# Half of an output projection by Strassen's seven products, in a new order of the stage's close

## The chip, the cores and the metric

The kernel runs on one core of one Trainium2 chip. Its metric is device time in microseconds (us); the time before is the median of three runs, 615.01 us (614.92 to 615.44). The core's engines have queues of their own and run beside each other: PE (TensorE, matrix products, with a loader for the stationary operand that the profile calls PEld), DVE (VectorE), ACT (ScalarE), POOL (GpSimd) and SP (SyncE, which here only issues transfers). In this kernel PE's products go into PSUM, used as eight banks of 128 x 512 floats, and DVE or ACT read them from there; POOL works on the other on-chip memory, SBUF.

## The reference, cut to what matters

512 tokens (8 sequences of 64) of width 512 go through three layers, each added to its input:

```python
x = x + xattn(layernorm(x), ctx, W, b)        # attention over 1601 context rows
x = x + attn(layernorm(x), ...)               # linear attention, then an MLP
x = x + ffn(layernorm(x), ...)                # 8 experts, top 2

# attn: 16 heads of 64, causal
h = _ln(x, g1, beta1)
q = elu((h @ wq) @ proj) + 1;  k = elu((h @ wk) @ proj) + 1;  v = h @ wv
out_t = sum_{s<=t} (q_t . k_s) v_s / (sum_{s<=t} q_t . k_s + 1e-6)
x = x + out @ wo                              # out: 512 x 1024, wo: 1024 x 512
x = x + gelu(_ln(x, g2, beta2) @ w1 + b1) @ w2 + b2
```

The change is about `x + out @ wo`. Everything is in 32-bit floats.

## The kernel before, in words

The kernel is written in a layer (Tile) that inserts the semaphores between engines. With `manual_schedule` every engine, SP's queue too, runs its instructions in the order of the program text, so the order of the Python calls below is the order of each queue. Two things come on top of that. PSUM is two pools of four banks, `mm_bank` and `acc_bank`; a new bank is the one of its pool that came free first, by the order planned when the program is built, and its first writer waits for the last reader of the tile that had it. Big inputs stream through a ring of 12 buffers of 1 MB: `stream` lists them in order, `issue_to` issues transfers up to a place in that list as long as the oldest of the 12 has been marked done (`done`), `need` asks for one and looks `AHEAD` = 6 further, and `scratch` takes a ring buffer for intermediate results.

The linear attention works on pairs of heads, j = 0 to 7, 128 channels each. Per pair:

- `linear(which, i)` projects q or k for two pairs by Strassen's seven quarter products (PE; copies on ACT L782; sums on POOL L786), with sums of weight quarters made by `sum_weights` (POOL, L719 to L722).
- `features(j)` (L821) multiplies by `proj` into two "acc" banks, `pr_wq` and `pr_wk`; ACT (L832, L836) and DVE (L838) make phi of it. phi has one buffer for each of q and k.
- `products(j)` (L851) makes the scores of 64 by 64 blocks into two "mm" banks; DVE masks them (L860) into `masked`, which has two buffers, one for each head.
- `attend_j(j)` (L874, L884) multiplies by ones and by v, into two "acc" banks `nd`.
- `denominators` (ACT, L897) and `divide` (DVE: a reciprocal of 128 x 512, L904, and two products, L906) write the pair's 128 channels of `a_t`, 512 tokens wide. The products are the last readers of the `nd` banks.

The loop over j is staggered: in round j come linear(j), attend_j(j-3), products(j-2), divide(j-3), features(j-1). So three rounds are left for the close. There the output product is worked in between: `output(t, js)` (L946) multiplies `a_t[:, j, tile t]` by the j-th 128 rows of wo, 512 columns wide, for four tiles t of 128 tokens, and adds up eight j in one PSUM bank. Before, its calls come in the order

```python
output(0, range(4)); rest = features(7); rest(0); rest(1); products(6)
output(1, range(2)); divide(5, attend_j(5)); output(1, [2, 3]); output(0, [4])
both = attend_j(6); products(7); divide(6, both); output(1, [4])
output(0, [5]); output(1, [5]); divide(7, attend_j(7)); output(2, range(6))
output(0, [6, 7]); output(1, [6, 7])   # then the joins
```

`join(t)` (DVE, L981) adds a tile's bank to the residual `xin` and takes its statistics (L983), `normal(t)` (L993) normalizes it, `turn_h2(t)` (PE, L1007) transposes it, and ACT (L996) or, for tile 2, DVE (L999) scales it. Tile 2's last two matmuls, and the whole of tile 3, stand between these. `sum_tokens` (POOL for the first tile of each half, DVE for the second, L581 to L584) makes the sums of h2 that the MLP's Strassen products need; `first_products`, `second_products` and `fifth` (L1042) are the first of these on PE. `first_products(0)` is called right behind tile 3's last output matmul, and join(3) behind it.

In the close POOL makes the sums of the first two w1 blocks (`sum_weights("w1", 0)` and 1) and of four pairs of w2 rows (`sum_down`, L745 to L748), which are used later; it is then idle until sum_tokens.

At the very start, `NIDLE` = 23 products of the identity with itself (L237) are run before there is any data; the first `NARROW` = 13 are 8 columns wide, the other ten 128.

Of the kernel before, what the change touches and what calls it, by code (L numbers as in the profile page):

```python
# [17 lines left out]
ALU = mybir.AluOpType  # L18
AX = mybir.AxisListType

P = 128
B, S, D = 8, 64, 512
# [18 lines left out]
NBIG = 7  # L41
LN_EPS = 1e-5
RING = 12
NIDLE = 23
NARROW = 13
AHEAD = 6


# [1 line left out]
def perceiver_kernel(  # L50
# [22 lines left out]
    nc = tc.nc  # L73
# [45 lines left out]
    half = H * DH // 2  # L119
# [57 lines left out]
    place = {key: i for i, (key, _) in enumerate(order)}  # L177
# [30 lines left out]
    def done(*keys):  # L208

        freed.update(keys)  # L210
# [514 lines left out]
    HD = D // 2  # L725
    scratches, dsums, hsums = {}, {}, {}

    def sums_tile(name, i):

        if (name, i // 2) not in scratches:  # L730
            scratches[name, i // 2] = scratch(f"{name}_{i // 2}")
        return scratches[name, i // 2][1][:, 2 * (i % 2) : 2 * (i % 2) + 2, :].rearrange(
            "p a (b n) -> p (a b) n", b=2
        )

    def down_part(i, row, half):

        f = 2 * i + row
        return streamed["w2", f // 4][:, f % 4, half * HD : (half + 1) * HD]

    def sum_down(i):

        s = sums_tile("dsum", i)
        t1, t2, t3, t4 = dsums[i] = [s[:, k, :] for k in range(4)]
        nc.gpsimd.tensor_tensor(t1, down_part(i, 0, 1), down_part(i, 0, 0), ALU.subtract)  # L745
        nc.gpsimd.tensor_tensor(t2, down_part(i, 1, 1), t1, ALU.subtract)
        nc.gpsimd.tensor_tensor(t3, down_part(i, 1, 1), down_part(i, 0, 1), ALU.subtract)
        nc.gpsimd.tensor_tensor(t4, down_part(i, 1, 0), t2, ALU.subtract)  # L748

    if True:  # L750
        a_t = la1.tile([P, H * DH // P, B * S], F32, name="a_t")
# [63 lines left out]
        def features(j):  # L815

            pr = {which: acc_bank(f"pr_{which}_{j}") for which in ("wq", "wk")}
            for r in range(2):
                rows = slice(r * DH, (r + 1) * DH)
                for which, other in (("wq", r), ("wk", 1 - r)):  # L820
                    nc.tensor.matmul(  # L821
                        pr[which][other * DH : (other + 1) * DH, :],
                        proj2[rows, :],
                        lin[which, j][rows, :],
                        start=True,
                        stop=True,
                    )
# [12 lines left out]
            return rest  # L840

        def products(j):


            banks_ = [mm_bank(f"qk_{j}_{r}") for r in range(2)]
            for t in range(NT):
                for h in range(2):
                    cols = slice(t * P + h * S, t * P + (h + 1) * S)
                    for r in range(2):
                        rows = slice(r * DH, (r + 1) * DH)  # L850
                        nc.tensor.matmul(  # L851
                            banks_[r][h * S : (h + 1) * S, t * S : (t + 1) * S],
                            phi["wk", j][rows, cols],
                            phi["wq", j][rows, cols],
                            start=True,
                            stop=True,
                        )
# [35 lines left out]
        def denominators(j, both):  # L893

            rden = la2.tile([P, 2, NT * S], F32, tag="rden", name=f"rden_{j}")
            for h in range(2):
                nc.scalar.activation(rden[:, h, :], both[h][:, NT * S :], AF.Identity, bias=tiny)  # L897
            return rden

        def divide(j, both, rden=None):  # L900

            if rden is None:
                rden = denominators(j, both)
            nc.vector.reciprocal(rden, rden)  # L904
            for h in range(2):
                nc.vector.tensor_tensor(  # L906
                    a_t[:, j, :].rearrange("p (t h q) -> p t h q", t=NT, h=2)[:, :, h, :],
                    both[h][:, : NT * S].rearrange("p (t q) -> p t q", t=NT),
                    rden[:, h, :].rearrange("p (t q) -> p t q", t=NT),
                    ALU.mult,  # L910
                )

        halves_of = [(which, i) for i in range(nj // 2) for which in ("wq", "wk")]
# [22 lines left out]
        for i in range(2):  # L936
            sum_weights("w1", i)
        for i in range(ND):
            sum_down(i)
        wo_banks = {}  # L940

        def output(t, js):
            if t not in wo_banks:
                wo_banks[t] = (mm_bank if t < 3 else acc_bank)(f"wo_{t}")
            for j in js:
                nc.tensor.matmul(  # L946
                    wo_banks[t],
                    a_t[:, j, t * P : (t + 1) * P],
                    wo_r[j // 4][:, j % 4, :],
                    start=(j == 0),  # L950
                    stop=(j == nj - 1),
                )

        output(0, range(4))
        rest = features(nj - 1)
        for k in range(2):
            rest(k)
        products(nj - 2)
        output(1, range(2))
        divide(nj - 3, attend_j(nj - 3))  # L960
        output(1, range(2, 4))
        output(0, [4])
# [12 lines left out]


        h2n, h2_t = v_sb[:, :, :D], v_sb[:, :, D:]
# [55 lines left out]
    mlp2 = mid.enter_context(tc.tile_pool(name="mlp2", bufs=2))  # L1033
# [1088 lines left out]
```

## Time and profile before

| what | before |
|---|---|
| median of three runs | 615.01 us (614.92 to 615.44) |
| profiled execution | 615.04 us, its span 613.3 us |
| mean granted clock of PE | 0.996 |
| PE busy | 599.7 us, 3820 instructions |
| DVE, ACT, POOL busy | 185.7, 151.2, 176.1 us |
| output product L946 | 64 matmul instructions of 128 x 512, 237.0 to 272.6 us |
| reciprocals L904 | 8 of 128 x 512, 3.34 us each |

The span runs from the first to the last instruction of one execution. A line of the timeline gives start, busy time, engine, source line, operation, output <- inputs, form and count; what stands in brackets is how long the engine had been idle before it and what ended that. A 32-bit matmul is two PE instructions, each with a load of its own on PEld, and the start-to-start distance of these in a run, not their listed duration, is what a matmul costs. Busy time of an engine says nothing by itself of what sets the end: a line counts if PE, or what PE waits for, would be later by it.

### The profile page before, as it was taken

To read this page: it belongs to the slowest core of one execution; us is meant where nothing else is said; L and a number is where in the kernel's file an instruction comes from. 1 tells how busy PE (TensorE), PEld (TensorE's weight loads), DVE (VectorE), ACT (ScalarE), POOL (GpSimd) and SP (SyncE) were. 2 spreads that over 40 slices of the span, in tenths; PEclk is the share of its full clock that TensorE was granted. 3 is DMA by queue.
4 is the path that set the end of the run, shared out by engine and by line. 5 is a ranking of instruction groups with operands and counts; after the bars stand their busy time and mean duration, and the time that the engine had idled before them with its cause. 6 is when DMAs were issued, how large, how long until landed. Compare 5 with 4: busy or idle time off the path is not lost. (4 is left out here: it accounts for less than half of the span.)

```text
span 613.3 us, 9571 instructions
## 1 busy us (share of the span) xinstructions
PE 599.7 (98%) x3820; PEld 394.4 (64%) x3820; DVE 185.7 (30%) x448; ACT 151.2 (25%) x317; POOL 176.1 (29%) x241
## 2 busy tenths in 40 slices
PE   8999999999999999999999999999999999999994
PEld 7543434343477775558888658939763848776793
DVE  4121414234402667865104245412212011101100
ACT  3241313140136665233112311301101101101110
POOL 4000000000188758415996021332300111301111
PEclk9999999999999999999999999999999999999998
DMA  8999999999822003001336414158860778775611
GB/s 333 418 418 421 418 419 415 421 418 409 341 70 69 1 3 138 2 1 34 105 138 261 151 69 149 64 162 320 286 253 1 266 270 292 287 286 179 276 20 17
DMA packets 23942, 131.87 MB, mean 215 GB/s; under 512 B 4372, under 2 KB 4372, under 8 KB 12488
## 3 DMA queue, kind: packets, MB, share of 16 engines
q1 hardware_dynamic: 19496, 122.36, 50.8%
q0 software_dynamic: 3280, 7.61, 5.1%
q10 hardware_dynamic: 1104, 1.07, 0.5%
q8 instruction: 40, 0.66, 0.4%
q14 instruction: 22, 0.18, 0.1%
HBM read 126.08 MB, written 4.94 MB: 214 GB/s over the span
## 5 line engine op out<-in xcount | busy, mean ns | idle before, releaser
L1619 PEld LDWEIGHTS up<-xgT,e_up 128*128 128x128 f32 x896 | 100.7, 192 | 4.5 <-ACT y_sb L1597 2.5
L1619 PE MATMUL up<-xgT,e_up 128*128 128x128 f32 x896 | 101.6, 276 | 1.0 <-PEq L1952 0.6
L1598 POOL DMA_INDIRECT out_dram<-y_sb,dst_late x12 | 18.3, 1526 | 167.8 <-ACT y_sb L1597 97.7
L1585 DVE TENSOR_TENSOR mid<-up,act 128x256 f32<-128x256 f32 x38 | 16.1, 425 | 150.5 <-ACT act L1583 150.5
L1633 PE MATMUL y<-e_wo,mid 128*128 128x512 f32 (+1 forms) x144 | 58.8, 548 | 0.0
L472 PE MATMUL sc<-ctxT,pw_t 128*64 128x401 f32 (+1 forms) x256 | 47.5, 503 | 0.0
L1583 ACT ACTIVATE act<-up 128x256 f32<-128x256 f32 x38 | 14.6, 383 | 119.3 <-PE up L1619 97.1
L533 PE MATMUL av<-ctx,eT 128*64 128x512 f32 x192 | 43.5, 595 | 0.0
L581 POOL TENSOR_TENSOR h_sums<-h_t 128x256 f32<-128x256 f32 x1 | 0.7, 724 | 144.1 <-PE avt L560 144.1
L1633 PEld LDWEIGHTS y<-e_wo,mid 128*128 128x128 f32 x144 | 25.7, 190 | 20.5 <-issue 17.8
L472 PEld LDWEIGHTS sc<-ctxT,pw_t 128*64 128x64 f32 x256 | 18.6, 136 | 27.2 <-issue 24.3
L1042 PE MATMUL side<-v_sb,sum_w 128*128 128x256 f32 x128 | 30.5, 380 | 0.2 <-DVE v_sb L581 0.2
L533 PEld LDWEIGHTS av<-ctx,eT 128*64 128x64 f32 x192 | 13.6, 137 | 25.3 <-issue 24.9
L946 PE MATMUL wo<-wo,a_t 128*128 128x512 f32 x64 | 29.2, 601 | 0.0
L618 PE MATMUL v<-wv,h_t 128*128 128x512 f32 x64 | 29.1, 597 | 0.0
L904 DVE RECIPROCAL rden<-rden 128x512 f32<-128x512 f32 x8 | 26.7, 3343 | 0.2 <-ACT rden L897 0.2
L1042 PEld LDWEIGHTS side<-v_sb,sum_w 128*128 128x128 f32 x128 | 24.2, 190 | 3.9 <-issue 0.6
L1127 PE MATMUL mlp<-w,hid_sb 128*128 128x512 f32 (+1 forms) x50 | 22.3, 584 | 0.0
L480 ACT ACTIVATE scores<-sc,pb 128x401 f32<-128x401 f32 (+1 forms) x16 | 9.5, 591 | 46.6 <-PE sc L472 46.6
L618 PEld LDWEIGHTS v<-wv,h_t 128*128 128x128 f32 x64 | 11.6, 190 | 13.4 <-issue 13.0
L489 DVE TENSOR_REDUCE negmax<-scores 128x1 f32<-128x1601 f32 x4 | 7.3, 1821 | 42.5 <-ACT scores L480 42.5
L946 PEld LDWEIGHTS wo<-wo,a_t 128*128 128x128 f32 x64 | 11.5, 190 | 13.2 <-issue 11.0
(353 smaller groups left out, 917.3 us busy)
## 6 DMA issues: line engine op xcount, KB each, us to landing
e_up<-in_L_ffn_up_dram SPq DMA_DIRECT2D x32, 1024.0 KB, 6.0
ctx<-in_ctx_dram SPq DMA_DIRECT2D x24, 1024.0 KB, 15.7
ctxT<-in_ctx_T_dram SPq DMA_DIRECT2D x24, 802.0 KB, 13.8
e_wo<-in_L_ffn_wo_dram SPq DMA_DIRECT2D x16, 1024.0 KB, 10.1
w<-in_L_attn_w_dram SPq DMA_DIRECT2D x8, 1024.0 KB, 8.3
ctxT<-in_ctx_T_dram SPq DMA_DIRECT2D x8, 796.0 KB, 15.3
wv<-in_L_attn_wv_dram SPq DMA_DIRECT2D x2, 1024.0 KB, 14.0
wq<-in_L_attn_wq_dram SPq DMA_DIRECT2D x2, 1024.0 KB, 15.6
```

Source lines behind the costliest of these rows:

```text
L472: nc.tensor.matmul(sc[h * S : (h + 1) * S, :width], pw_t[:, c, (2 * t + h) * S : (2 * t + h + 1) * S], keys[h][:, c, :], start=(c == 0), s ...
L533: nc.tensor.matmul(av[h * S : (h + 1) * S, :], e_t[:, 4 * g + j, h * S : (h + 1) * S], rows[h][:, j, :], start=(g == 0 and j == 0), stop=F ...
L618: nc.tensor.matmul(bank, h_t[:, c, t * P : (t + 1) * P], wv_n[:, c, :], start=(c == 0), stop=(c == KC - 1))
L904: nc.vector.reciprocal(rden, rden)
L946: nc.tensor.matmul(wo_banks[t], a_t[:, j, t * P : (t + 1) * P], wo_r[j // 4][:, j % 4, :], start=(j == 0), stop=(j == nj - 1),)
L1042: nc.tensor.matmul(bank[:, :HT], weights[:, c, :], rows[:, c, :], start=(first and c == 0), stop=(c == 1), skip_group_check=True,)
L1127: nc.tensor.matmul(acc[t][:, part], hid[:, t * P : (t + 1) * P], w[:, part], start=False, stop=(f == FF // P - 1), skip_group_check=True,)
L1583: nc.scalar.activation(act, bank[:, :FQ], AF.Silu)
L1585: nc.vector.tensor_tensor(hid, bank[:, FQ:], act, ALU.mult)
L1598: nc.gpsimd.indirect_dma_start(out=out, out_offset=bass.IndirectOffsetOnAxis(ap=dst[:n, :], axis=0), in_=y_sb[:n, :], in_offset=None, boun ...
L1619: nc.tensor.matmul(bank[:, m * P : (m + 1) * P], up_of[q][:, c, m * P : (m + 1) * P], xg_t[c], start=(c == 0), stop=(c == KC - 1),)
L1633: nc.tensor.matmul(bank[:, :width], h_t[:, j * P : (j + 1) * P], w[:, 2 * (q % 2) + j, n * width : (n + 1) * width], start=(q + j == 0), s ...
```

## The change

The first four of the eight j (two pairs of j, `NS` = 2) are multiplied by wo by Strassen's seven products instead of eight. With two j as the inner halves, two halves of 256 tokens as rows and two halves of 256 columns of wo, each product is, for one pair and one tile of 128 tokens, a matmul of 256 columns.

- Four sums of wo's quarters (`sums_of_output`) and four of a_t's (`sum_attended`) for each pair, all on POOL and in rounds 4 to 7 of the loop, into two buffers of the ring ("wo_sums") that are listed with no source.
- Products 1, 5, 6, 7 (`output_shared`) go to a bank each and serve more than one output quarter. ACT copies each to a part of `h_t`, whose old content is no longer needed, and POOL adds them to the residual `xin` in seven adds of 128 x 512. Product 7 takes an "acc" bank, the others "mm" banks.
- Products 2, 3, 4 (`output_alone`) go straight to the output banks. The last four j are multiplied as before, `output(t, [4..7])`.
- The order of the close is new: products(7) comes ahead of attend_j(6), tile 2's and tile 3's product 4 comes after chunk 7 of tiles 0 and 1, and only four chunks of tile 3 stand between the turns.
- `sum_weights("w1", ...)` and `sum_down` on POOL move behind or between the new sums and adds.
- `NIDLE` goes from 23 to 11 and `NARROW` from 13 to 1: ten wide ones remain, and one narrow one.

```diff
-NIDLE = 23
-NARROW = 13
+NIDLE = 11
+NS = 2
+NARROW = 1
...
     for r in range(2):
         stream(("wo", r), wo[r])
+    for i in range(NS):
+        stream(("wo_sums", i), None)
...
+    def columns_sums(part, outs, which=range(4)):
+        t1, t2, t3, t4 = outs
+        for k in which:
+            dst, a, b = (
+                (t1, part(0, 1), part(0, 0)),
+                (t2, part(1, 1), t1),
+                (t3, part(1, 1), part(0, 1)),
+                (t4, part(1, 0), t2),
+            )[k]
+            nc.gpsimd.tensor_tensor(dst, a, b, ALU.subtract)
...
+        def sums_of_output(i, which=range(4)):
+            if len(wo_sums) == i:
+                issue_to(place["wo_sums", i] + 1)
+                s = streamed["wo_sums", i]
+                parts_ = [s[:, k // 2, k % 2 * HD : (k % 2 + 1) * HD] for k in range(8)]
+                wo_sums.append(parts_[:4])
+                at_sums.append(parts_[4:])
+            columns_sums(lambda row, half: wo_part(i, row, half), wo_sums[i], which)
...
+        def sum_attended(i):
+            s1, s2, s3, s4 = at_sums[i]
+            even, odd = a_t[:, 2 * i, :], a_t[:, 2 * i + 1, :]
+            nc.gpsimd.tensor_tensor(s1, even[:, HT:], odd[:, HT:], ALU.add)
+            nc.gpsimd.tensor_tensor(s2, s1, even[:, :HT], ALU.subtract)
+            nc.gpsimd.tensor_tensor(s3, even[:, :HT], even[:, HT:], ALU.subtract)
+            nc.gpsimd.tensor_tensor(s4, odd[:, :HT], s2, ALU.subtract)
...
+            if j in (nj - 4, nj - 3):
+                sums_of_output(0, range(2) if j == nj - 4 else range(2, 4))
+            if j == nj - 2:
+                sum_attended(0)
+                sums_of_output(1)
+            if j == nj - 1:
+                sum_attended(1)
             if j > 2:
                 both = attend_j(j - 3)
...
+        def output_alone(k):
+            rows, weights = {
+                2: (lambda i: block(i, 1, 0), lambda i: wo_part(i, 1, 0)),
+                3: (lambda i: at_sums[i][3], lambda i: wo_part(i, 1, 1)),
+                4: (lambda i: block(i, 1, 1), lambda i: wo_sums[i][3]),
+            }[k]
+            half = int(k == 3)
+            for t in range(2):
+                output(t + 2 * (k == 4), range(NS), slice(half * HD, (half + 1) * HD), rows, weights)
...
+        def output_shared(k, pairs):
+            if k not in wo_shared:
+                wo_shared[k] = (acc_bank if k == 7 else mm_bank)(f"wo_shared_{k}")
+            for i in pairs:
+                rows = {1: block(i, 0, 0), 5: at_sums[i][0], 6: at_sums[i][1], 7: at_sums[i][2]}[k]
+                weights = {1: wo_part(i, 0, 0), 5: wo_sums[i][0], 6: wo_sums[i][1], 7: wo_sums[i][2]}[k]
+                for t in range(2):
+                    nc.tensor.matmul(
+                        wo_shared[k][:, t * HD : (t + 1) * HD],
+                        rows[:, t * P : (t + 1) * P],
+                        weights,
...
+        def copy_shared(k):
+            nc.scalar.copy(wo_copies[k], wo_shared[k].rearrange("p (t n) -> p t n", t=2))
...
+        output_shared(1, every)
+        copy_shared(1)
+        sum_weights("w1", 0)
+        add((0, 0), p1)
+        rest = features(nj - 1)
+        output_shared(5, every)
+        for k in range(2):
+            rest(k)
+        copy_shared(5)
+        output_shared(6, [0])
+        products(nj - 2)
+        both = attend_j(nj - 3)
+        rden = denominators(nj - 3, both)
+        output_shared(6, range(1, NS))
+        copy_shared(6)
+        sum_weights("w1", 1)
+        add(p6, p1)
+        add(p5, p6)
+        add((0, 1), p5)
+        add((1, 1), p5)
+        add((1, 0), p6)
+        divide(nj - 3, both, rden)
+        output_shared(7, every)
+        copy_shared(7)
+        add((1, 0), p7)
+        add((1, 1), p7)
         for i in range(ND):
             sum_down(i)
...
+        products(nj - 1)
         both = attend_j(nj - 2)
-        products(nj - 1)
         divide(nj - 2, both)
-        output(1, [4])
+        output_alone(2)
+        output_alone(3)
         for t in range(2):
-            output(t, [5])
+            output(t, [4])
         divide(nj - 1, attend_j(nj - 1))
...
-        output(2, range(6))
         for t in range(2):
-            output(t, [6, 7])
+            output(t, [5])
+        output(2, [4, 5])
+        for j in (6, 7):
+            for t in range(2):
+                output(t, [j])
+        output_alone(4)
...
         of = join(2)
-        output(3, range(3))
+        output(3, [4, 5])
         normal(2, *of)
         turn_h2(0, [by_act])
         turn_h2(1, [by_act])
-        output(3, range(3, nj - 2))
+        output(3, [6])
         turn_h2(2, [by_dve])
-        output(3, range(nj - 2, nj))
+        output(3, [7])
+        done(*[("wo_sums", i) for i in range(NS)])
```

More of the change, by code (lines that the diff above doesn't have):

```diff
@@ L743, in sum_down @@
         s = sums_tile("dsum", i)
[L744 to L748, printed above, removed]
+        dsums[i] = [s[:, k, :] for k in range(4)]
+        columns_sums(lambda row, half: down_part(i, row, half), dsums[i])
     if True:
@@ L911, in divide, with wo_part @@
                 )
+        wo_sums, at_sums = [], []
+        def sums_of_output(i, which=range(4)):
[6 more added lines that the diff above has]
+            columns_sums(lambda row, half: wo_part(i, row, half), wo_sums[i], which)
+        def wo_part(i, row, half):
+            j = 2 * i + row
+            return streamed["wo", j // 4][:, j % 4, half * HD : (half + 1) * HD]
+        def sum_attended(i):
[5 more added lines that the diff above has]
+            nc.gpsimd.tensor_tensor(s4, odd[:, :HT], s2, ALU.subtract)
         halves_of = [(which, i) for i in range(nj // 2) for which in ("wq", "wk")]
@@ L935, in perceiver_kernel, with output @@
         done(*[(which, n) for which in ("wq", "wk") for n in range(2)])
-        for i in range(2):
-            sum_weights("w1", i)
+        wo_banks = {}
+        def output(t, js, part=slice(0, D), rows=None, weights=None):
+            start = t not in wo_banks
+            if start:
+                wo_banks[t] = (mm_bank if t < 3 else acc_bank)(f"wo_{t}")
+            for j in js:
+                if rows is None:
+                    row, weight = a_t[:, j, t * P : (t + 1) * P], wo_r[j // 4][:, j % 4, :]
+                else:
+                    row, weight = rows(j)[:, t % 2 * P : (t % 2 + 1) * P], weights(j)
+                nc.tensor.matmul(
+                    wo_banks[t][:, part],
+                    row,
+                    weight,
+                    start=(start and j == js[0]),
+                    stop=(rows is None and j == nj - 1),
+                    skip_group_check=True,
+                )
@@ new lines, in block @@
+        def block(i, row, side):
+            return a_t[:, 2 * i + row, side * HT : (side + 1) * HT]
+        def output_alone(k):
[7 more added lines that the diff above has]
+                output(t + 2 * (k == 4), range(NS), slice(half * HD, (half + 1) * HD), rows, weights)
@@ new lines, in perceiver_kernel @@
+        wo_shared = {}
+        def output_shared(k, pairs):
[5 more added lines that the diff above has]
+                for t in range(2):
+                    nc.tensor.matmul(
+                        wo_shared[k][:, t * HD : (t + 1) * HD],
+                        rows[:, t * P : (t + 1) * P],
+                        weights,
+                        start=(i == 0 and t == 0),
+                        stop=(i == NS - 1),
+                        skip_group_check=True,
+                    )
@@ new lines, in perceiver_kernel, with add @@
+        wo_copies = {k: h_t[:, n, :].rearrange("p (t n) -> p t n", t=2) for n, k in enumerate((1, 5, 6, 7))}
+        def copy_shared(k):
+            nc.scalar.copy(wo_copies[k], wo_shared[k].rearrange("p (t n) -> p t n", t=2))
+        def add(dst, other):
+            if isinstance(dst, tuple):
+                side, half = dst
+                dst = xin[:, 2 * side : 2 * side + 2, half * HD : (half + 1) * HD]
+            nc.gpsimd.tensor_tensor(dst, dst, other, ALU.add)
+        p1, p5, p6, p7 = (wo_copies[k] for k in (1, 5, 6, 7))
@@ new lines, in perceiver_kernel @@
+        every = range(NS)
+        output_shared(1, every)
[14 more added lines that the diff above has]
+        sum_weights("w1", 1)
@@ L938, in perceiver_kernel @@
+        add(p6, p1)
[8 more added lines that the diff above has]
+        add((1, 1), p7)
         for i in range(ND):
             sum_down(i)
[L940 to L962, printed above, removed]
+        products(nj - 1)
         both = attend_j(nj - 2)
-        products(nj - 1)
         divide(nj - 2, both)
-        output(1, [4])
+        output_alone(2)
+        output_alone(3)
         for t in range(2):
-            output(t, [5])
+            output(t, [4])
```

## The prediction

> **What bounds the kernel now.** The page comes first: one engine is busy nearly all the time.
>
> ```profile
> PE 599.7 (98%) x3820; PEld 394.4 (64%) x3820; DVE 185.7 (30%) x448; ACT 151.2 (25%) x317; POOL 176.1 (29%) x241
> ```
>
> So only what lengthens or shortens PE's own queue counts. Busy times by stretch of the stage's close (PE, PEld, DVE, ACT, POOL, then clock, DMA share, GB/s) say the same of the place of the change:
>
> ```profile
> 237.00:240.80 3.80, 3.71 (x12) 1.44 (x8) 3.77 (x3) 2.12 (x4) 3.72 (x6) 1.00 1.03 431
> 242.20:245.87 3.67, 3.65 (x80) 2.10 (x77) 1.31 (x3) 2.12 (x4) 3.51 (x6) 1.00 0.02 9
> 254.05:272.64 18.59, 18.59 (x59) 8.93 (x54) 13.56 (x25) 6.00 (x15) 0.62 (x1) 1.00 0.00 1
> ```
>
> PE has no holes, DVE is second. Then the order in time of PE and DVE there, and the waits of features' line:
>
> ```profile
> 237.01 3.70 PE L946 MATMUL wo<-wo,a_t 128*128 128x512 f32 x8
> 240.84 0.61 PE L821 MATMUL pr_wq<-lin_wq,proj 64*64 64x512 f32 x1
> 241.17 0.61 PE L821 MATMUL pr_wk<-lin_wk,proj 64*64 64x512 f32 x1
> 242.27 0.69 PE L851 MATMUL qk<-phi_wq,phi_wk 64*64 64x64 f32 x32
> ```
> ```profile
> 236.89 3.34 DVE L904 RECIPROCAL rden<-rden 128x512 f32<-128x512 f32 x1
> 240.27 0.76 DVE L906 TENSOR_TENSOR a_t<-nd,rden 128x256 f32<-128x256 f32 x2
> ```
> ```profile
> L821 PEldq EVENT_SEMAPHORE  x11: 51/51/51, 182.5 to 241.1; - x11
> ```
>
> This is the line to remember: features(7) starts its wq half just after divide(4)'s first product (240.27 + 0.42 = 240.69) and its wk half just after the second (241.03); PE's loader waited on a semaphore at 241.1. Its two "acc" banks are those of attend_j(4), which divide(4) reads last, and divide(4) hangs on a reciprocal that DVE starts at 236.89. Before, PE's eight wo instructions (237.01 to 240.71) just filled that time.
>
> **Part 1: fewer columns.** The wo product is 64 instructions (two per matmul) of 512 columns; their loads in a run are 0.43 us apart, so 0.857 us a matmul, 32 x 0.857 = 27.4. Half width is on record in the Strassen projection:
>
> ```profile
> 215.24 0.84 PEld L770 LDWEIGHTS wk<-h_t,sum_wk 128*128 128x128 f32 x4
> 216.10 0.84 PEld L770 LDWEIGHTS wk<-h_sums,wk 128*128 128x128 f32 x4
> ```
>
> Four instructions in 0.86, so 0.43 a half-width matmul. After: 16 full (13.7) and 28 half (12.0) = 25.7. Gain 1.7 us.
>
> **Part 2: where it lies.** Ahead of features(7) stood 4 full matmuls (3.43); now 4 half ones, output_shared(1) (1.71). Behind it stand 28 x 0.857 = 24.0 before, and 16 x 0.857 + 24 x 0.43 = 24.0 now. The whole gain is in front of features(7), and that is pinned by divide(4), which nothing upstream moves: masked(5), rden(4), DVE's queue are as before. PE will be done with output_shared(1) at 237.01 + 1.71 = 238.7 and idle 2.1 us until 240.8. Parts 1 and 2 together: 0.
>
> **Part 3: from 242.2 to the MLP.** I lay PE's new queue out with the old durations: 32 small products 0.63, an attend_j 1.06, a switch from full-width wo to the small ones 0.2, from half width 0.1 (216.32 + 0.86 to 217.27).
> - output_shared(5) and the first pair of (6), 2.66, to 244.8; products(6) and attend_j(5), 1.6, to 246.4 (end of attend_j(5) before: 245.9). phi(7) may overwrite phi(6) only after products(6), so DVE's phi(7) moves from 243.9 to 245.5, masked(6) to 246.9, divide(5)'s reciprocal from 246.88 to 247.6, done 251.0, its products to 251.8.
> - The rest of (6) and (7), 2.66, to 249.1; products(7) to 249.8, attend_j(6) to 250.8. Its second bank is that of output_shared(7), free after ACT's copy (0.59) at 249.7: no stall. This is a choice, see rival A.
> - output_alone(2), (3) and chunk 4 for two tiles: 3.4 + 1.7 + 0.2, to 256.1. DVE meanwhile: masked(7) 251.8, reciprocal 252.5 to 255.9, divide(6) 256.7. attend_j(7) to 257.2; ACT 0.84; reciprocal 258.1 to 261.45; a_t(7) 262.2. PE has six full matmuls in that time, 5.14, to 262.3: just enough, 0.1 to spare.
> - Chunk 7 twice, output_alone(4), six more full ones and three turns (0.99 and 0.45): 1.71 + 1.71 + 5.14 + 1.6, to 272.4, against 272.64 before. h2n(1) is ready 4.7 after tile 0's last matmul (261.2 to 265.9 before), 268.1, its turn at 269.3; h2n(2) 2.8 after that join begins (268.1), 270.9, its turn at 271.05. Fits, the last by 0.1. Sum -0.2.
> - Behind the last turn stands only one matmul (0.86) where there were two. DVE's four scalings of it (1.37) now end after PE, at 273.2, so join(3) starts at 273.2 and not 272.84: +0.4; normal(3) and its turn follow, where before PE reached that turn 0.2 after it was ready. Net on fifth(0), which waited on that chain before (0.2): **+0.3**.
>
> **Part 4: POOL.** Before it has these holes:
>
> ```profile
> 230.81 1.59 POOL L786 TENSOR_TENSOR lin_wk<-lin_wk,first_wk 128x256 f32<-128x256 f32 x2 [3.58 <-ACT lin_wk L782]
> 272.02 0.72 POOL L581 TENSOR_TENSOR v_sb<-v_sb 128x256 f32<-128x256 f32 x1 [18.99 <-DVE v_sb L999]
> ```
>
> At j = 4 and 5 two more ops each, 0.7 apart (dsum: four in 2.87): the next adds start 0.6 late and catch up. At j = 6 eight more, 5.7, from 227.2 to 233.0, where 3.6 was free: linear(7)'s adds end 0.9 late, the one features(6) needs at 236.0, when PE comes at 235.96. At most 0.2, and it falls into the 2.1 us hole; so does anything up to 2. In the close: sum_attended(1) 2.9, seven adds of 128x512 at 1.26 (the residual adds of the MLP) 8.8, then the old eight and sixteen sums. From 236.8, with one wait for the copy of (6) at 248.1, POOL is done at 268.3, 4 us before sum_tokens; the adds join(0) needs are done by 253, the last by 257. Cost 0; POOL more than 4 us later would hold fifth(0), which reads sum_tokens' results, one for one.
>
> **Part 5: small things.** Four copies of 0.59 on ACT, which is busy a third of the time here (12.6 of 36.7): 0, and 0.6 each if ACT were full. Two ring buffers for wo_sums push two loads of w1, w2 from 152 on to the release of wv and wq (171.6 and 192.4, where two others were issued before), two to 234.7, w1_3 to about 256, w2_3 to about 275; SP's queue is held at each, with nothing behind it but w's until e_up at 288. They land 8.3 us later; first uses are 264 (sum_down), 294, 327 and 346. Cost 0.
>
> **Part 6: the start.** 24 narrow idle instructions go:
>
> ```profile
> L237 PE MATMUL idle<-ident 128*128 128x128 f32 x20 | 4.6, 429 | 0.0
> L237 PE MATMUL idle<-ident 128*8 128x8 f32 x26 | 0.8, 172 | 1.4 <-POOL ident masks.py:199 1.4
> ```
>
> 0.03 us each, so the wide ones end at 6.1, not 6.83, and PE idles 0.8 us before the first transposes, which wait for DVE at 6.93. The wide ones run at 0.23 each; the same shape in the query (32 in 3.81) at 0.12: PE runs at half rate until about 7. If the hole kept it there for as long again as the idle block (5.4 us), 23 of the 44 instructions before 12.45 would be done by 12.3 and the rest by 14.8; the keys' second half lands at 13.21, so +1.6. The other end is 0, and not below: DVE sets 6.93. I take 0, as the wide ones are all kept. [...]
>
> The 2.1 us hole of part 2 has the same two ends: 0, or 5.4 us at half rate, +2.7. No PE hole in this trace is like it; PE ran on at full pace after 0.9 us waits, so 0. [...]
>
> **Sum.** 0 + 0.3 + 0 + 0 = +0.3 on the profiled execution's 615.04 (span 613.3 and 1.7 around it), which is the median 615.01 within 0.03: **615.3**, no change by the 0.2% (1.2 us) that a measurement of this kernel can tell.
>
> **Rivals.**
> - A, slower: attend_j(6)'s second bank is attend_j(5)'s, as features(7)'s were attend_j(4)'s. It is free after divide(5)'s first product, 251.4, where PE comes at 249.8: stall 1.6, then masked(7), which overwrites what attend_j(6) reads, and all after it. 616.9. It decides if the order of banks puts that product before ACT's copy of (7); on the chip's own times the copy is 1.7 us earlier. The e_up load at 326.7, which waited for dsum's buffer (last add 326.4) while w2_1's had been free since 321, shows that the plan's order is not always the chip's.
> - B, slower: the clock after one of the holes, +1.6 or +2.7: 616.9 to 618.
> - C, faster: features(7) does not wait for divide(4). Then 1.7 comes through: 613.6. Against it stand the semaphore at 241.1 and the 0.33 us between pr_wq and pr_wk.
>
> **How the numbers follow.** Forecast 0.55, A 0.20, B 0.12, C 0.13. The forecast's own range is 614.3 to 616.4, from the DVE chain's 0.1 spare and the four switches at 0.2; I give it 0.45 within the bound, 0.05 beyond it on either side. Faster 0.13 + 0.05, same 0.45, slower 0.05 + 0.20 + 0.12. The range 613.9 to 617.3 leaves out most of C and the far end of B, some 0.17.
>
> **What would show it.** Right: a hole of about 2 us on PE before pr_wq near 238.7, released by a_t; features(7) at 240.8 as before; first side product near 272.4, join(3) near 273.2. A: a hole before nd near 250 released by a_t. B: 128-column matmuls at 0.23 after 7 us. C: pr_wq at 238.8. Wrong would be a new wait of PE on POOL's sums, or of join on POOL's adds.

## The result, and the profile after

The changed kernel took 616.46 us (median of 13 runs, 615.66 to 617.77) beside 615.01 for the kernel before (13 runs, 614.74 to 615.44): a ratio of 1.0027, 95% interval 1.0020 to 1.0034. That is slower, by a little more than a measurement can tell, and 1.2 us above the forecast of 615.3, inside its range (613.9 to 617.3). The 13 times fall into two groups, and the result can't be understood without this: eight lie between 615.66 and 616.65, five between 617.65 and 617.77, and the kernel before has no such second group. The mean granted clock of the five is 0.992 to 0.993, that of the others 0.995 to 0.996, but for the 616.65 (0.993).

The execution profiled for the changed kernel is one of the lower group, 616.09 us with a span of 614.4. Its busy times from the page:

```profile
PE 597.1 (97%) x3820; PEld 396.7 (65%) x3820; DVE 186.4 (30%) x448; ACT 153.6 (25%) x321; POOL 197.0 (32%) x265
```

PE works 2.6 us less than before (599.7). About 1.0 of that is the idle matmuls, and the rest is near the 1.7 forecast for the output product; yet the span is 1.1 longer. The stretch from the first shared product to the last features (PE, PEld, DVE, ACT, POOL, clock, DMA share, GB/s):

```profile
236.72:240.56 3.84, 2.00 (x13) 1.47 (x9) 3.81 (x3) 2.60 (x5) 3.68 (x7) 1.00 0.99 420
```

PE is busy for 2.00 of 3.84 us here, where it was full before. The order in time of PE there, and of DVE:

```profile
236.72 1.99 PE L1022 MATMUL wo_shared<-wo,a_t 128*128 128x256 f32 x8
240.56 0.61 PE L833 MATMUL pr_wq<-lin_wq,proj 64*64 64x512 f32 x1 [1.84 <-DVE a_t L918]
```
```profile
236.61 3.34 DVE L916 RECIPROCAL rden<-rden 128x512 f32<-128x512 f32 x1
239.99 0.76 DVE L918 TENSOR_TENSOR a_t<-nd,rden 128x256 f32<-128x256 f32 x2
```

Against the start of features(6), features(7) comes 4.86 us later, as before (4.85). The four full matmuls that filled this time are four half ones now, and the rest is a hole of 1.84 us, put down to `a_t`. So the saving has gone where the prediction put it. Further down, the close of the stage shows what it had not named. DVE's normals of tiles 0 and 1 and the join behind them, and POOL's last subtraction for the down weights:

```profile
267.00 1.06 DVE L1108 TENSOR_SCALAR v_sb<-xin,mv_h,rstd_h 128x512 f32<-128x512 f32 x1
268.16 0.76 DVE L1108 TENSOR_SCALAR v_sb<-xin,mv_h,rstd_h 128x512 f32<-128x512 f32 x1
268.85 0.68 DVE L1096 TENSOR_TENSOR xin<-wo,xin 128x512 f32<-128x512 f32 x1
```
```profile
267.73 0.91 POOL L741 TENSOR_TENSOR dsum<-w,dsum 128x256 f32<-128x256 f32 x1
```

The two normals in the kernel before:

```profile
264.66 0.55 DVE L993 TENSOR_SCALAR v_sb<-xin,mv_h,rstd_h 128x512 f32<-128x512 f32 x1
265.31 0.55 DVE L993 TENSOR_SCALAR v_sb<-xin,mv_h,rstd_h 128x512 f32<-128x512 f32 x1
```

normal(0) and normal(1) took 0.55 each before; now they take 1.06 and 0.76, while POOL, moved back by its new work, is at its last subtractions for the down weights (until 268.64). The next join, at 268.85, is late by that, and PE's turn of tile 2 waits for normal(2):

```profile
271.78 0.63 PE L1122 MATMUL tr_h<-ident,v_sb 128*128 128x128 f32 x4 [0.38 <-DVE v_sb L1108]
```

The first fifth product, before and now:

```profile
278.61 4.55 PE L1042 MATMUL side<-v_sb,sum_w 128*128 128x256 f32 x20 [0.20 <-DVE v_sb L581]
```
```profile
279.10 4.55 PE L1158 MATMUL side<-v_sb,sum_w 128*128 128x256 f32 x20
```

From the first product of features(6) to there it was 42.62 us before (235.99 to 278.61) and is 43.40 now (235.70 to 279.10): +0.78. The start gave 0.29 back, so PE is 0.49 late at 279. It stays so until 550, where one wait at a branch in the last stage is 0.77 us and was 0.43 (before, and now):

```profile
550.36 3.64 PE L1671 MATMUL up<-e_up,xgT 128*32 128x512 f32 x32 [0.43 <-ACTq L1950]
```
```profile
551.21 2.35 PE L1787 MATMUL up<-e_up,xgT 128*32 128x512 f32 x20 [0.77 <-ACTq L2066]
```

That makes 0.84; the end of the span, behind the last output rows' issue, adds 0.2, and the span is 1.1 longer. The second group of times is 1.6 us above this.

### The profile page after: what moved, and what is told of

It is laid out like the page before. It is cut to its first block, busy times and chain, and to the rows that moved or that the text cites. A ratio compares the mean times of both kernels' runs of the same rounds, so it can differ in the third digit from the quotient of the medians.

```text
span 614.4 us, 9601 instructions
## 1 busy us (share of the span) xinstructions
PE 597.1 (97%) x3820; PEld 396.7 (65%) x3820; DVE 186.4 (30%) x448; ACT 153.6 (25%) x321; POOL 197.0 (32%) x265
## 5 line engine op out<-in xcount | busy, mean ns | idle before, releaser
L1660 POOL DMA_INDIRECT xg<-mn_dram,src_late x16 | 16.6, 1034 | 10.6 <-DVE dst_late L1654 5.7
L1181 ACT ACTIVATE hid_sb<-hid_sb,col 128x256 f32<-128x256 f32 (+1 forms) x16 | 9.8, 615 | 29.8 <-DVE hid_sb L1215 21.0
```

The source lines that it names most:

```text
L1660: nc.gpsimd.indirect_dma_start(out=xg[:n, :], out_offset=None, in_=mn_dram, in_offset=bass.IndirectOffsetOnAxis(ap=slots[key][0][:n, :], a ...
```

## The experiments

All of them ran beside the kernel before. Its medians were 615.16 (27 runs), 615.04 (16), 614.95 (27) and 614.81 (15) in the four sets, and each ratio is to the runs of its own set. Where medians of two sets are subtracted below, their kernels before differ by up to 0.35 us.

### Which part makes the second group: the start or the hole

Two edits, alone and together: the idle matmuls of the start as they were, and the fifth shared product in the hole.

```diff
-NIDLE = 11
-NARROW = 1
+NIDLE = 23
+NARROW = 13
```
```diff
+        output_shared(5, every)
         rest = features(nj - 1)
-        output_shared(5, every)
```

The changed kernel with the old start:

> The changed kernel with the idle matmuls of the start as they were before (23, of which 13 narrow). Its times had fallen into two groups, 615.66 to 616.65 and 617.65 to 617.77, some 1.6 us apart, the kernel before's into one. Start theory: the second group is a TensorE clock that comes to full rate later when the first matmuls leave holes; then this kernel has one group only, at 615.7 to 616.7, median about 616.2. Hole theory: the second group is the clock falling after the 1.84 us hole ahead of the last features; then both groups stay, in about the same shares (5 of 13 in the upper), median 616.1 to 617.7. In both, the new close itself still costs its 0.5 to 0.8 us, and the kernel stays above 615.5.

The kernel before with the new start:

> The kernel before with the new start alone (11 idle matmuls, one narrow). Start theory: two groups, about 614.9 and 616.6, the upper in a third of the runs. Hole theory: one group, at 614.7 to 615.4 as before, or 0.3 to 0.7 below it, since the profiled execution of the changed kernel was 0.7 us ahead at 20 us and 0.28 ahead at the last features but one.

The changed kernel with the hole filled, and with both edits:

> The changed kernel with the fifth shared product moved ahead of the last features, so that TensorE has 1.72 us of products where it had its 1.84 us hole. Theory of the prediction (the saved 1.7 us went into that hole, because the last features wait for the division of chunk 4): everything from the last features' products on comes 1.7 earlier, median 1.5 to 1.8 us below the changed kernel's, the lower group at about 614.4. Rival (the chain on VectorE or GpSimd through the close, phi to reciprocal to a_t to join, is what sets the end, and the hole is only where the slack shows): under 0.4 us gained. Start theory: still two groups, 614.4 and 616.0. Hole theory: one group, at 614.4.

> Both edits: the start as before and the hole filled. Start theory and theory of the prediction: one group at about 614.4, 0.6 us below the kernel before. Hole theory: the same as with the hole filled alone. If neither the hole nor the start matters, 616.2 and 617.7 as the changed kernel.

| kernel | median, us | runs | ratio (95%) |
|---|---|---|---|
| after_old_start | 618.27 (617.45 to 620.25) | 5 | 1.0050 (1.0036 to 1.0064) |
| before_new_start | 615.47 (615.03 to 615.74) | 11 | 1.0004 (0.9995 to 1.0013) |
| after_filled | 614.38 (614.23 to 614.77) | 11 | 0.9987 (0.9978 to 0.9996) |
| after_filled_old_start | 615.75 (614.70 to 617.88) | 11 | 1.0014 (1.0005 to 1.0023) |

The start theory falls: the new start alone leaves the kernel before as it was, in one group. The hole theory holds for after_filled: with the hole filled there is one group, 0.54 us wide. If each of the 11 executions had had the chance of the unfilled ones (5 of 13, and 2 of 5 with the old start, so 7 of 18), none in 11 would come about once in 200 times (11/18 to the 11th power). after_filled_old_start is less clean: its times are spread over 3 us, and one of its 11 executions, 617.88 at a mean clock of 0.994, may have had such a fall; no profile shows what it was, and profiles without a fall have 0.995 to 0.997, by when the clock drops behind the last product (at 608.57 us in the kernel before, 609.44 in the changed one). One profile, that of after_old_start, caught the clock falling. The order in time of its PE:

```profile
240.86 0.61 PE L833 MATMUL pr_wq<-lin_wq,proj 64*64 64x512 f32 x1 [1.84 <-DVE a_t L918]
242.39 4.31 PE L1022 MATMUL wo_shared<-wo_sums 128*128 128x256 f32 x12
```

and its stretches of a microsecond (the clock is the third figure from the right):

```profile
241.00:242.00 1.00, 1.00 (x8) 0.24 (x7) 1.00 (x3) 0.00 (x0) 1.00 (x2) 0.98 0.24 98
242.00:243.00 1.00, 1.00 (x5) 0.52 (x3) 0.24 (x1) 0.52 (x2) 1.00 (x2) 0.50 0.04 16
243.00:244.00 1.00, 1.00 (x4) 0.82 (x3) 0.00 (x0) 1.00 (x4) 1.00 (x2) 0.50 0.00 0
244.00:245.00 1.00, 1.00 (x4) 0.82 (x3) 0.00 (x0) 0.60 (x2) 0.92 (x3) 0.50 0.00 0
245.00:246.00 1.00, 1.00 (x5) 0.83 (x5) 0.00 (x0) 0.13 (x1) 1.00 (x2) 0.82 0.00 0
```

Half rate from 241.96 to 245.38 (0.89 of full clock in the slice 241.8 to 242.0, 0.58 in 245.2 to 245.4). The twelve instructions of shared products take 4.31 us instead of 2.86, the features 1.53 instead of 1.34 (to the start of the next product): 1.64 us in all, which is the distance of the two groups (617.76 and 616.12 in the middle). Such a fall takes 3.42 / 2 / 616 = 0.0028 off the mean clock, as the upper group has it. For the changed kernel itself no profile fell into that group. The clock records of the traces show more: all stretches at full clock ahead of a fall, the one behind the last product included, last a whole number of times 3.413 us (600.75 us is 176 of them in the kernel before, 604.16 is 177 in the changed one, and these two differ by 3.413; 175 to 177 in all, here 69 and 108), and the first begins between 5.28 and 11.05 us. So in these traces the clock changed on a grid of 3.413 us that begins at another time in each execution (7.83 us before, 5.28 in the changed kernel), and the same hole can fall differently on it.

With the hole filled (after_filled), the products lie against each other:

```profile
238.60 1.89 PE L1022 MATMUL wo_shared<-wo_sums 128*128 128x256 f32 x8
240.59 0.61 PE L833 MATMUL pr_wq<-lin_wq,proj 64*64 64x512 f32 x1
```

That brings 2.08 us against the changed kernel's median, 1.74 against the middle of its lower group, and in the traces 1.75 in the stretch from features(6) to the first fifth product (43.40 to 41.65): so the 1.7 us of part 1 come through when something fits into the time before features(7). The hole was where they had gone, and not a sign of slack elsewhere.

The old start did what neither theory said: 1.4 us slower with the hole filled. The waits of PE behind it, from after_old_start's order in time:

```profile
502.05 3.64 PE L1787 MATMUL up<-e_up,xgT 128*32 128x512 f32 x32 [1.69 <-PEq L2066]
532.56 0.63 PE L1689 MATMUL xgt<-ident,xg 128*128 128x128 f32 x4 [1.01 <-issue]
```

Both stand in the last stage, 500 us after the edit. In the changed kernel the first wait was 0.48 and there was no second.

### What the old start costs: where it stands, or what it does

Three kernels put other work into the hole, so that the start stays short and PE's program gets longer; a fourth takes the kernel before and lengthens its start. By the position theory the wait goes with how many of PE's instructions stand ahead of the branch (1.69 us in after_old_start); its rival is that the old start's narrow matmuls cost the time themselves. The first, after_hole_wide, has four products (after_hole_half two):

```diff
+        wo_shared[5] = mm_bank("wo_shared_5")
+        for i in range(4):
+            nc.tensor.matmul(wo_shared[5], a_t[:, 0, :P], wo_r[0][:, i, :], start=True, stop=True, skip_group_check=True)
         rest = features(nj - 1)
```

> The changed kernel with four redundant 128x512 products (0.43 us each, 1.72 together) in its hole ahead of the last features; their bank is overwritten afterwards, so nothing of the result changes and no work is saved. Clock theory (the hole of 1.84 us lets the TensorE clock fall to half for 3.4 us in some executions, as one profile showed from 241.96 to 245.38): one group of times, the lower one of the changed kernel, median 616.1, none over 617. Rival (the upper group has to do with something else in the close, such as the GpSimd adds against VectorE): both groups stay, 616.1 and 617.7.

> The same with two such products, which leaves a hole of about 1.0 us. If a share of idle time in one 3.4 us window decides, and 1.84 of 3.4 us is just enough, 1.0 is not: one group at 616.1. If any hole of about a microsecond can do it: some executions at 617.7, fewer than 5 of 13.

In after_hole_narrow the loop is over 12 products of `ident[:, :8]` with itself. By the position theory this brings a wait of PE for its own sequencer of 1.3 us or more near 498, and 617.3 to 618.5; by its rival no such wait, and 616.1 to 616.9:

> The changed kernel with the twelve 8-column idle matmuls, that it had taken from the start, put into its hole instead (24 matmul records of 0.06 to 0.12 us, 1.4 to 2.8 us). The start stays the short one, and all instructions of TensorE behind the hole stand as far down the program as with the old start. [...]

The kernel before with `NIDLE = 35`, `NARROW = 25`:

> The kernel before with twelve more of the 8-column idle matmuls at its start (35, of which 25 narrow; 24 matmul records). They cost the start some 0.6 us: the twelve ended the row at 6.83 instead of 6.23. Position theory: the waits that the changed kernel had with twelve more come here too, since the change itself adds as many matmul records (24) ahead of the last stage as it takes from the start: a wait for TensorE's sequencer of 1.3 us or more near 499, and 616.7 to 617.3. Rival (the waits belong to the changed close, through the timing of its transfers or GpSimd): no such wait, 615.2 to 615.8.

| kernel | median, us | runs | ratio (95%) |
|---|---|---|---|
| after_hole_wide | 619.12 (618.77 to 619.23) | 5 | 1.0066 (1.0052 to 1.0080) |
| after_hole_half | 617.94 (617.31 to 619.18) | 5 | 1.0052 (1.0038 to 1.0066) |
| after_hole_narrow | 617.26 (616.13 to 617.60) | 6 | 1.0034 (1.0022 to 1.0047) |
| before_longer | 616.32 (615.42 to 617.08) | 11 | 1.0021 (1.0012 to 1.0030) |

The first two expectations missed, for two reasons. A 128x512 product here is two instructions and costs 0.86 us, not 0.43: the two of after_hole_half fill the hole (to 240.43, features(7) at 240.55) and the four of after_hole_wide run 1.55 past it (features(7) at 242.11). And both have a new wait in the last stage, 1.6 us in the one and here in the other:

```profile
531.12 1.98 PE L1752 MATMUL y<-e_wo,mid 128*128 128x512 f32 x4 [1.38 <-issue]
```

With these, 616.1 + 1.4 = 617.5 and 616.1 + 1.55 + 1.6 = 619.25 are to be expected, where 617.94 and 619.12 were measured. None of these 16 executions with a filled or a shorter hole (1.16 us is left in after_hole_narrow) had a mean clock below 0.995, so the clock theory stands. Beside the 617.88 above, two more of the kernels with a filled hole had a lower one (0.994 at 614.97 in after_filled_pool, 0.989 at 616.38 in after_filled_two_short); what lowered it no profile shows.

The position theory held in both of its tests, by the waits in the traces. after_hole_narrow, whose median lies at the lower edge of what was expected (617.3 to 618.5), has the short start and its instructions in the hole, and shows the old start's wait:

```profile
500.20 3.64 PE L1790 MATMUL up<-e_up,xgT 128*32 128x512 f32 x32 [1.53 <-PEq L2069]
```

The kernel before, which has nothing of the change, shows it when its start is as much longer, with a wait of the second kind too:

```profile
499.54 3.64 PE L1671 MATMUL up<-e_up,xgT 128*32 128x512 f32 x32 [1.53 <-PEq L1950]
529.88 0.63 PE L1573 MATMUL xgt<-ident,xg 128*128 128x128 f32 x4 [0.83 <-issue]
```

Its 616.32 is 0.4 below what was expected (616.7 to 617.3). The first wait came in all four kernels with 24 more matmul records (1.37 to 1.69); the second is 0.24 in after_hole_narrow and missing in after_filled_old_start. The four kernels with 24 more matmul records ahead of the last stage (after_old_start, after_filled_old_start, after_hole_narrow, before_longer) are the four whose first instruction queue moves 41 packets instead of 40. That row for the changed kernel, and for after_old_start:

```profile
q8 instruction: 40, 0.66, 0.4%
```
```profile
q8 instruction: 41, 0.67, 0.4%
```

That the 41st packet makes the wait is not shown: the row does not say which engine a packet is for, nor what waits for it. The first wait stands at a branch of the last stage (L2066 is the `If` on the number of tokens); the second is put down to `issue`, which names no branch. That the waits of after_hole_wide and after_hole_half, at another place, come from the same cause is not shown either.

So the change's trimmed start has a use that the prediction did not see: it takes 24 matmul records from the program, as many as the Strassen products add.

### ScalarE's wait at 551

```diff
-        nc.scalar.activation(warm2, eps, AF.Sqrt)
+        for _ in range(5):
+            nc.scalar.activation(warm2, eps, AF.Sqrt)
```

> The kernel before with four more one-column activations of ScalarE (0.20 us each, in its wait of 6.3 us before the first standard deviation), as the new close adds four to ScalarE's instructions with its copies. In the changed kernel TensorE waits 0.77 us for ScalarE's sequencer near 551 where it waited 0.43, and this stays through every variant of it. Position theory for ScalarE: 0.77 here too, and 615.2 to 615.5. Rival (the gathers' timing, or the close's own work): 0.43, and 614.8 to 615.1.

615.23 us (11 runs, 614.89 to 615.53), a ratio of 1.0004 (0.9995 to 1.0013), and the wait is there, in a kernel without the change:

```profile
550.95 3.64 PE L1672 MATMUL up<-e_up,xgT 128*32 128x512 f32 x32 [0.77 <-ACTq L1951]
```

The four activations themselves lie in a wait of ScalarE that is still 5.38 long. So the 0.35 us come with four more instructions in ScalarE's program, copies in the one kernel and activations in the other; the time alone, with its interval, could not tell it. Why they do is not shown: the rows of the instruction queues are the same as before in this run.

### GpSimd's subtractions against VectorE's normals

Both on top of the filled hole: of the sixteen subtractions for the down weights the last four, or the last two, move behind `sum_tokens` on POOL.

```diff
-        for i in range(ND):
+        for i in range(ND - 1):
             sum_down(i)
...
     sum_tokens(nc.gpsimd, h2_t, tsum, 0)
+    sum_down(ND - 1)
```

> The kernel with the hole filled by the fifth shared product, and the last four of GpSimd's sixteen subtractions for the down weights moved behind its sums of tokens, into its idle time from 276 on. Port theory (the two normals of VectorE took 1.06 and 0.76 us in place of 0.55 because GpSimd was subtracting at the same time, and the next join, normal and transposes are late by it): both normals back at 0.55, the first side product 0.4 to 0.7 us earlier, median 613.7 to 614.0. Rival (the join of tile 2 waits for TensorE's own products, not for the normals): the normals are shorter and the time stays within 0.2 of 614.4. Against it: the last normal (0.67 beside the sums of tokens) would meet the moved subtractions, up to 0.5 us.

For two, `sum_down(ND - 1, range(2))` stays and `sum_down(ND - 1, range(2, 4))` moves:

> The kernel with the hole filled by the fifth shared product, and only the last two of GpSimd's sixteen subtractions for the down weights moved behind its sums of tokens. With four moved, the normals were back at 0.55 us and the first side product 0.56 earlier against the last features, but the last two met VectorE's sums of tokens (0.94 in place of 0.42) and the gain was gone by 278. Port theory: two end GpSimd's run near 265.4, before the normals, and its second run by 276, before VectorE's sums; both normals and all four sums short, the fifth product 0.4 to 0.6 earlier, median 613.8 to 614.1. Rival (the sums of tokens wait for ScalarE's turn of tile 3 and TensorE's side products ahead of them, so that nothing arrives earlier than they let it): 614.3 to 614.5 again.

| kernel | median, us | runs | ratio (95%) |
|---|---|---|---|
| after_filled_pool | 614.48 (613.99 to 614.97) | 11 | 0.9990 (0.9981 to 0.9999) |
| after_filled_two | 613.64 (613.37 to 614.25) | 11 | 0.9980 (0.9971 to 0.9989) |

With four moved both normals are back at 0.55 and PE's first side product is 0.57 us earlier against features(7), and nothing is gained: DVE's sums of tokens then meet the moved subtractions.

```profile
276.88 0.94 DVE L585 TENSOR_TENSOR v_sb<-v_sb 128x256 f32<-128x256 f32 x1
```

With two moved, neither meets (after_filled_two, DVE's normals and the join behind them):

```profile
265.23 0.55 DVE L1109 TENSOR_SCALAR v_sb<-xin,mv_h,rstd_h 128x512 f32<-128x512 f32 x1
265.89 0.55 DVE L1109 TENSOR_SCALAR v_sb<-xin,mv_h,rstd_h 128x512 f32<-128x512 f32 x1
266.35 0.68 DVE L1097 TENSOR_TENSOR xin<-wo,xin 128x512 f32<-128x512 f32 x1
```

and the stretch from features(6) to the first fifth product is 41.10 us, against 41.65 with the hole filled alone, 43.40 in the changed kernel and 42.62 before. That is 0.55, as expected. The medians differ by 0.74, but they are of two sets, and against its own kernel before each gains 0.78 and 1.31: 0.53. The intervals of the two ratios overlap; the traces are what shows it. This kernel beats both, the kernel before by 0.20% and the changed one by 0.46% between medians.

### A still shorter start

On top of after_filled_two, `NIDLE = 7`, which takes 8 more matmul records from the front of PE's program. By the position theory that changes nothing or brings a new wait of 1 to 1.7 us at one branch; of the start this was expected:

> The same with 7 idle matmuls at the start in place of 11 (four wide ones less, 8 of TensorE's records). [...] The first matmuls would be ready 1.6 us earlier but wait for VectorE until 6.8 as before; if the clock then rises later, up to 1.6 us more at the start.

614.39 us (11 runs, 613.70 to 616.38), ratio 0.9993 (0.9984 to 1.0002). No new wait in the last stage, but the later clock that was held possible at the start: the first matmuls of the program run at about half their later rate for longer. The trace's clock record begins with full rate at 11.05 us, that of after_filled_two at 5.33. From its order in time:

```profile
7.40 1.92 PE L413 MATMUL w_t<-ident,w_sb 128*128 128x128 f32 x8
9.11 4.67 PE L401 MATMUL pw<-h_t,w_sb 128*128 128x128 f32 x32
```

These took 1.09 and 3.74 in after_filled_two, with eleven. It is not the number of idle matmuls alone: after_filled_pool, with eleven, took 1.91 and 4.26 in its profile, where full rate begins at 10.55. What it costs in the end is not shown: PE was 0.66 us later at 16, but no longer so at 98 (97.82 beside 97.85), and the profiled execution is 613.89 beside 613.73. Why the median is 0.75 higher stays open.

## Why the prediction was right or wrong, by its own steps

- **Fewer columns (part 1), -1.7.** Right: filling the hole brought 1.74 against the lower group, and 1.75 in the traces.
- **Where it lies (part 2).** Right to 0.3 us: there was a hole ahead of features(7) of 1.84 (2.1 was forecast), ended by `a_t`, with features(7) as late after features(6) as before. What such a hole costs beside its length was left to part 6.
- **The new close (part 3), +0.3.** The sum was +0.78. The part that was worked out from the order of the products is right: without the meeting of POOL and DVE it is 41.10 + 1.75 (what the filling took from the stretch, 43.40 - 41.65) = 42.85, so +0.23 against 42.62. The step that failed is the assumption that durations stay as they were: normal(0) and normal(1) went from 0.55 to 1.06 and 0.76, and the "fits, the last by 0.1" for tile 2's turn became a wait of 0.38. join(3) came at 273.74, not 273.2.
- **POOL (part 4), 0.** Its times were right (done at 268.64, forecast 268.3). The conclusion was wrong: POOL was asked only when it would be done, for those who wait for it, and not what runs on DVE at the same time. It cost 0.55, by the two traces with the hole filled.
- **Small things (part 5).** No wait for the loads of w1 and w2 arose, as forecast. The copies cost ScalarE nothing, but with its four more instructions there is 0.35 us more at a branch 300 us later, which no step asked about.
- **The start and the hole (part 6).** For the start 0 was right within what can be told: the new one alone gives 1.0004 (0.9995 to 1.0013). But the other end does occur: after_filled_pool, with the same start, ran at half rate until 10.55 in its profile, and had features(6) at 235.96, 0.26 behind the changed kernel. The hole was the step that failed. "PE ran on at full pace after 0.9 us waits, so 0" has no such row in the trace of before: behind the start PE's longest wait there is 0.58 (ahead of 478.76), a third of the hole. In 5 of 13 executions the price was 1.6 us, with a hole of 1.84. The other end of that step, 5.4 us at half rate, was too long: it was 3.42 in the one profile that has it.
- **Rivals.** A did not come: attend_j(6) follows products(7) without a wait.

```profile
249.00 0.69 PE L863 MATMUL qk<-phi_wq,phi_wk 64*64 64x64 f32 x32
249.51 0.67 PE L886 MATMUL nd<-masked,ones 64*64 64x256 f32 x5
```

C did not come: features(7) waits. B, given 0.12, is what 5 of 13 executions did, at the hole and at +1.6. The forecast took all executions to be alike.

Against the forecast's sum, the profiled execution's +0.75 is made of +0.55 (VectorE's normals beside GpSimd's subtractions), +0.35 (ScalarE's branch), +0.2 (the end of the span), -0.07 (the rest of part 3) and -0.29 (the start, which in this execution was early). The median is 0.4 above that execution, since five of thirteen stand in the upper group. The forecast itself, no change, was therefore wrong by a little: its mechanism held, and two prices of 0.35 to 0.55 and one of 1.6 in 5 of 13 executions were missing. The forecast's own range ended at 616.4; that the 616.46 lies inside the wider one is owed to the room given to rivals A and B, and A was not what happened.

## What to carry to other kernels

When work is taken from in front of a wait that something else pins, move other work into the gap with the same edit: here the gap kept the whole saving of 1.7 us, and in one profile the clock fell to half for 3.42 us behind a gap of 1.84. Before work is moved to another engine, look at what runs beside it at that time (here VectorE's normals beside GpSimd's subtractions, 1.06 and 0.76 us in place of 0.55), not only at when it is done. Here a few instructions more on TensorE, and on ScalarE, went with a longer wait at a branch hundreds of microseconds later (1.53 us instead of 0.48, and 0.77 instead of 0.43); in a program with branches, compare the waits of the branches in both profiles before a small difference is put down to the edit.

## What the runs showed of the hardware that was not expected

- The clock of TensorE fell to half for 3.42 us, 1.1 us after a hole of 1.84 us had ended, in one profile; by their times, some 7 of 18 executions with this hole had it. On the grid of 3.413 us the step that ended at 241.95 had begun at 238.54 and held the whole hole, 1.84 us or 54% of it, an estimate from one profile. The same share did not lower the clock in the changed kernel's profile: there the step from 237.39 to 240.80 holds the whole hole too (PE busy for 1.57 of 3.41 us), and the clock stayed full. What PE does in the rest of the step differs (1.09 us of it were the features' 64x64 products where the clock fell, 0.24 where it did not); that this matters is not shown. With 1.16 us left of the hole it was not seen in 6 executions.
- With twelve small matmuls more in TensorE's program PE waited 1.53 us instead of 0.48 at a branch of the last stage, in a kernel with and one without the change; with four instructions more for ScalarE another wait was 0.77 instead of 0.43.
- VectorE's normal of 128x512, one input from SBUF, took 1.06 and 0.76 us beside GpSimd's subtractions, and 0.55 without; its difference of two SBUF inputs took 0.94 in place of 0.42.
